# Output weights loaded piece by piece into the places of a finished activation, in a one-core AdaLN transformer block

## The chip, the cores and the metric

The kernel runs on one core of one Trainium2 chip. A core has TensorE (PE), which multiplies matrices, VectorE (DVE), ScalarE (ACT), GpSimd (POOL), and SyncE (SP), which here only issues DMA transfers. Each engine works through its own instructions in order, and they meet through semaphores. The metric is the device time of one execution in microseconds, lower being better.

## The reference

One adaptive-layernorm block over 2048 tokens of width 512, in fp32. A conditioning row `c` gives six rows of 512 numbers through `wmod`: `sa, ca, ga, sb, cb, gb`. Then

```python
h = layernorm(x) * (1 + ca) + sa
x = x + ga * attention(h)      # 16 heads of 128, causal; sum over heads of attn @ O_w, + O_b
h = layernorm(x) * (1 + cb) + sb
x = x + gb * experts(h)        # 64 experts, 4 per token, and two shared ones
```

`ga` and `gb` are first pushed away from zero (their magnitude is made at least 0.25). Only the attention half and the seam between the halves bear on this change.

## The kernel before

The normalised activation `hT` (512 x 2048, turned so that the width lies on partitions) is one tile of 4 MB. Attention runs over `steps` (L341): 16 heads of five steps each, written here as (head, step). A step s works on the query blocks `BATCHES[s]` (L339): 7; 6; 5 and 0; 4 and 1; 3 and 2, each of 256 queries. The order is written out by hand (`manual_schedule`): `merge` (L83) interleaves up to three streams of work by the columns of matmul that each holds, so that all come to their end together, and calls `marks` when a given share of the step has been issued. The streams of step n are

- the scores and softmax of step n+2 (`softmax_tile`, L368): matmuls of up to 1024 columns into `ps`, of which there are two buffers, the row maximum on DVE (L421), the exponential on ACT into `p` (L427), and later a normalisation on DVE (L397);
- the weighted values of step n (`weighted_values`, L463): matmuls of `v` with the turned probabilities `pt` into `po`, then a copy by ACT and a store by POOL's queue into the DRAM array `atd` (L489);
- fillers: the projections of the next head's k and q (`JOBS`, L343, 2048 columns each), the values of the next pair of heads (1024 each), and what a step adds.

At the end of a step `swap` (L595) issues 16 transfers on SP that exchange 32 x 32 block columns from `p` into `pt` (L451) for step n+2; at marks 0.55 and 0.8 of the next step DVE transposes the two halves of `pt` in place (L461). So a probability tile passes DVE, SP's queue, the DMA engines and DVE again before PE needs it.

Around the last two heads the kernel also prepares the second half of the block. The late rows `ga, sb, cb, gb` are made by `late_mod` (L525), four matmuls of 512 columns each from a 1 MB block of `wmod` that `load_mod` (L509) fetches: row 2 in step (14,4), rows 3 and 4 in (15,0), row 5 in (15,1). `gate` (L103) applies the magnitude rule, six DVE operations. The output weights `O_w` (4 MB) go to the place of `hT` once its last reader, `make_q` in (14,4), is done: in (15,0) POOL issues the loads of row 4's block, of `O_w` in four pieces (L631) and of row 5's block, and then multiplies the 16 heads' weights by `ga` (L636). `load_ab` (L539) fetches the stored attention of 15 heads for one block of 256 queries, and `begin_output(t)` (L555) sums 15 heads of output tile t (15 matmuls of 512 columns) into `parts[t]`; tiles 0 to 3 are made in steps (15,1) to (15,4). After the last step the head still missing is added for these four tiles (L896), and the other twelve tiles follow (L917).

Of the kernel before, what the change touches and what calls it, by code (L numbers as in the profile page):

```python
# [18 lines left out]
P = 128  # L19
# [4 lines left out]
def adaln_block_kernel(  # L24
# [99 lines left out]
    with ExitStack() as att:  # L124
# [1 line left out]
        acst = enter(tc.tile_pool(name="acst", bufs=1))  # L126
        psA = enter(tc.tile_pool(name="psA", bufs=2, space=PSUM))

        hT = hTp.tile([P, DC, N], F32, name="hT")
        causal = acst.tile([P, P], F32)  # L130
        make_causal_mask(nc, causal, mask_val=-1e30)
        qkb = acst.tile([P, 2, H], F32)
# [31 lines left out]
        def project(b, j, hd, pool, name):  # L164

            w = heads[hd][b]
            ps = psA.tile([P, 512], F32, name="pqk", tag="mm")
            for k in range(DC):
                nc.tensor.matmul(  # L169
                    out=ps,  # L170
                    lhsT=w[:, k, :],
                    rhs=hT[:, k, j * 512 : (j + 1) * 512],
                    start=(k == 0),
                    stop=(k == DC - 1),
                )
# [12 lines left out]
        with tc.tile_pool(name="pre", bufs=1) as pre, tc.manual_schedule():  # L188
# [92 lines left out]
            def place_x(b, half):  # L281
                tp = turns.pop((b, half))
                for j in range(2):
                    k = 2 * half + j
                    nc.scalar.activation(
                        hT[:, k, b * 512 : (b + 1) * 512], tp[:, j, :], AF.Identity,
                        scale=mod[1][:, k : k + 1], bias=mod[0][:, k : k + 1],
                    )

# [32 lines left out]
        def make_v(g, t):  # L322

            if t == 0:
                vts[g] = vp.tile([P, NT, HG * DH], F32, name="v")
            wv, vb = groups[g]
            ps = psA.tile([P, HG * DH], F32, name="pv", tag="mm")
            for k in range(DC):
                nc.tensor.matmul(  # L329
                    out=ps,  # L330
                    lhsT=hT[:, k, t * P : (t + 1) * P],
                    rhs=wv[:, k].rearrange("p i d -> p (i d)"),
                    start=(k == 0),
                    stop=(k == DC - 1),
                )
            nc.vector.tensor_add(vts[g][:, t, :], ps, vb)
# [9 lines left out]
            (("q", 3), ("v", 2), ("v", 3), ("v", 4)),  # L346
            (("q", 2), ("q", 0), ("v", 5)),
            (("q", 1), ("v", 6), ("v", 7)),
        )

        def blocks_of(s):
# [143 lines left out]
        def fillers(hd, s):  # L495
            out = []
            g = hd // HG
            for what, j in JOBS[s]:
                if what == "v":
                    if g + 1 < NG:  # L500
                        out.append((1024, lambda j=j: make_v(g + 1, (hd % HG) * NP + j)))
                elif hd + 1 < H:
                    f = make_k if what == "k" else make_q
                    out.append((2048, lambda j=j, f=f: f(hd + 1, j)))
            return out

        mods = {}

        def load_mod(i, queue):  # L509

            if i == 3:
                mods[i] = [ktp.tile([P, 512], F32, name="kt") for _ in range(DC)]
            elif i in (2, 4):
                both = [vow.tile([P, DC, HG, DH], F32, name="wv") for _ in range(2)]
                both = [w.rearrange("p k i d -> p (k i d)") for w in both]
                mods[i] = [both[k // 2][:, (k % 2) * D : (k % 2 + 1) * D] for k in range(DC)]
            else:
                four = [qkw.tile([P, DC, DH], F32, name=("wq", "wk")[k % 2]) for k in range(DC)]
                mods[i] = [w.rearrange("p k d -> p (k d)") for w in four]
            for k in range(DC):  # L520
                queue.dma_start(
                    out=mods[i][k], in_=wmod[k * P : (k + 1) * P, i * D : (i + 1) * D]
                )

        def late_mod(i, dst):  # L525

            pm = psA.tile([P, D], F32, name="pm", tag="mm")
            for k in range(DC):
                nc.tensor.matmul(
                    out=pm, lhsT=silc[:, k, :], rhs=mods[i][k], start=(k == 0), stop=(k == DC - 1)  # L530
                )
            if i == 4:
                nc.vector.tensor_scalar_add(dst, pm, 1.0)
            else:
                nc.vector.tensor_copy(dst, pm)

        abs_ = {}

# [16 lines left out]
        def begin_output(t):  # L555
# [4 lines left out]
            def one(hd):  # L560
                if hd == 0:
                    box.append(psA.tile([P, D], F32, name="psb", tag="mm"))
                nc.tensor.matmul(
                    out=box[0],
                    lhsT=abs_[t // 2][:, hd, (t % 2) * P : (t % 2 + 1) * P],
                    rhs=wo[:, hd, :],
                    start=(hd == 0),
                    stop=(hd == H - 2),
                )
# [32 lines left out]
        with tc.manual_schedule():  # L602
# [9 lines left out]
            for n, (hd, s) in enumerate(steps):  # L612
# [3 lines left out]
                    if hd % HG == 1 and hd // HG + 2 < NG:  # L616
                        groups[hd // HG + 2] = load_group(hd // HG + 2)
                fill = fillers(hd, s)
                if hd == H - 2 and s == 3:
                    load_mod(2, nc.sync)  # L620
                    load_mod(3, nc.sync)
                if hd == H - 2 and s == 4:
                    load_ab(0)
                    fill.append((2048, lambda: late_mod(2, ga)))
                if hd == H - 1 and s == 0:
                    mag = qkw.tile([P, DC, DH], F32, name="wq")
                    gate(mag.rearrange("p k d -> p (k d)"), ga)
                    load_mod(4, nc.gpsimd)
                    wo = hTp.tile([P, H, D], F32, name="hT")
                    for i in range(0, H, 4):  # L630
                        nc.gpsimd.dma_start(  # L631
                            out=wo[:, i : i + 4, :], in_=O_w[i : i + 4].rearrange("h p d -> p h d")
                        )
                    load_mod(5, nc.gpsimd)
                    for i in range(H):
                        nc.gpsimd.tensor_mul(wo[:, i, :], wo[:, i, :], ga)  # L636
                    fill += [
                        (2048, lambda i=i, dst=dst: late_mod(i, dst))
                        for i, dst in ((3, sb), (4, cb))
                    ]  # L640
                if hd == H - 1 and s == 1:
                    rest = [vow.tile([P, DC, HG, DH], F32, name="wv") for _ in range(2)]
                    rest = [w.rearrange("p (j k) i d -> p j (k i d)", j=2) for w in rest]
                    nc.sync.dma_start(out=rest[0][:, 0], in_=O_b.partition_broadcast(P))
                    for t in range(NE):
                        load_x_tile(t)
                    fill.append((2048, lambda: late_mod(5, gb)))
                if hd == H - 1 and s == 2:
                    gate(rest[1][:, 0], gb)
                if hd == H - 1 and s >= 1:  # L650
                    if s == 2:
                        place = pp.tile([P, PW], F32, name="p")[:, : (H - 1) * 2 * P]
                        load_ab(1, place.rearrange("p (h t) -> p h t", t=2 * P))
                    if s == 3:
                        load_ab(2)
                    if s == 4:
                        nc.vector.tensor_copy(ga, rest[0][:, 1])
                        nc.sync.dma_start(out=last3, in_=atd[H - 1, :, : (NE - 1) * P])
                        nc.sync.dma_start(out=ones, in_=atd[H - 1, :, (NE - 1) * P : NE * P])
# [227 lines left out]
    with tc.manual_schedule():  # L887
# [6 lines left out]
        for t in range(NE):  # L894
# [1 line left out]
            nc.tensor.matmul(  # L896
                out=ps,
                lhsT=last3[:, t * P : (t + 1) * P] if t < NE - 1 else ones,
                rhs=wo[:, H - 1, :],
                start=True,  # L900
                stop=True,
            )
# [3 lines left out]
        for t in range(NE, NT):  # L906
# [9 lines left out]
            for hd in range(H):  # L916
                nc.tensor.matmul(  # L917
                    out=ps,
                    lhsT=abs_[pr][:, hd, i * P : (i + 1) * P],
                    rhs=wo[:, hd, :],  # L920
                    start=(hd == 0),
                    stop=(hd == H - 1),
                )
# [423 lines left out]
```

## Time and profile before

| What | Value |
|---|---|
| Device time, median of 3 runs | 2510.37 us (2509.43 to 2513.41) |
| Profiled execution, device time | 2493.62 us |
| Profiled execution, span on the core | 2491.8 us |
| Mean granted TensorE clock there | 0.994 |
| PE, DVE, ACT, POOL busy | 2419.3, 1514.8, 656.0, 249.2 us |
| DMA volume, mean rate | 326.25 MB, 131 GB/s |
| L896 begins (end of attention) | 1772.2 us after the span's start |

All views are of the one profiled execution; its time is set beside its span, and the runs without the profiler are the ones that are compared between kernels. An engine's busy share is a mean over stages, so the page's 40 slices and shorter windows are read before the totals. In a timeline, the brackets after a line give the idle time of the engine just ahead of it and the event that ended it.

### The profile page before, as it was taken

Reading aid. Unit: us, or ns where it says so; the run is one execution under the profiler, and the core shown is the slowest. Engines: PE = TensorE matmul, PEld = TensorE weight load, DVE = VectorE, ACT = ScalarE, POOL = GpSimd, SP = SyncE. Lnnn points to the kernel's source line nnn. Section 1 sums busy time; section 2 is a strip of 40 time slices with the busy share of each in tenths; the row PEclk is TensorE's granted clock in tenths of the full one; section 3 lists DMA queues with packets and bytes.
Section 4 is the critical chain, followed back from the end, with each engine's and each line's share of the span. In section 5 each row is a group of like instructions: output and inputs, shape, how many; then the busy total and the mean of one; then the engine's idle time right before and its main releaser. Section 6 shows DMA issues by size and latency. Waiting matters only on the chain.

```text
span 2491.8 us, 26256 instructions
## 1 busy us (share of the span) xinstructions
PE 2419.3 (97%) x8525; PEld 1526.6 (61%) x8525; DVE 1514.8 (61%) x2966; ACT 656.0 (26%) x1476; POOL 249.2 (10%) x314
## 2 busy tenths in 40 slices
PE   7999999999999999999999999979999999999999
PEld 4666666666666666666666666545554476876844
DVE  4566666666666666666666666565465572553664
ACT  3233233332333323333233333221111221222200
POOL 0000000000000000000000000041000021111164
PEclk9999999999999999999999999989999999999999
DMA  4234434444344443444444444475524266878665
GB/s 140 62 91 107 116 95 110 107 103 109 90 121 102 97 120 94 112 111 103 109 97 121 104 101 108 109 227 135 164 81 152 89 180 209 250 213 251 198 191 161
DMA packets 224399, 326.25 MB, mean 131 GB/s; under 512 B 32100, under 2 KB 140680, under 8 KB 224264
## 3 DMA queue, kind: packets, MB, share of 16 engines
q1 hardware_dynamic: 195656, 246.96, 38.4%
q0 software_dynamic: 19392, 60.84, 8.1%
q10 hardware_dynamic: 9216, 16.78, 1.8%
q8 instruction: 69, 1.13, 0.2%
q14 instruction: 66, 0.54, 0.1%
HBM read 139.91 MB, written 41.94 MB: 73 GB/s over the span
## 4 chain that ended last, share of the span: by engine, by line
PE 67%; DVE 17%; SPq 6%; DMA 4%; issue 4%; ACT 1%; DVEq 0%; POOL 0%; ACTq 0%; POOLq 0%
PE pqk L169 12%; PE ps L408 12%; PE po L479 9%; DVE pt L461 7%; PE pso L917 6%; SPq L451 6%; PE pv L329 5%; PE pst L1064 5%; PE pse L1209 4%; PE psd L1126 4%; DVE nm L421 4%; DMA pt<-p 3%; PE psg L980 3%; DVE p L397 3%; PE psy L1230 2%
## 5 line engine op out<-in xcount | busy, mean ns | idle before, releaser
L427 ACT ACTIVATE p<-ps,nm 128x1024 f32<-128x1024 f32 (+7 forms) x384 | 331.9, 864 | 1040.5 <-DVE nm L425 368.4
L408 PE MATMUL ps<-kt,qt 128*128 128x512 f32 (+3 forms) x1280 | 535.2, 535 | 43.0 <-ACT p L427 42.1
L479 PE MATMUL po<-pt,v 128*128 128x256 f32 (+1 forms) x2304 | 567.5, 369 | 7.0 <-DVE pt L461 3.6
L479 PEld LDWEIGHTS po<-pt,v 128*128 128x128 f32 x2304 | 426.4, 191 | 220.3 <-issue 155.8
L421 DVE TENSOR_REDUCE nm<-ps 128x1 f32<-128x1024 f32 (+7 forms) x384 | 349.6, 910 | 91.1 <-PE ps L408 82.4
L461 DVE STREAM_TRANSPOSE pt<-pt 128x1664 f32<-128x1664 f32 (+2 forms) x160 | 318.0, 1988 | 64.2 <-DMA pt<-p 59.9
L408 PEld LDWEIGHTS ps<-kt,qt 128*128 128x128 f32 x1280 | 235.5, 191 | 193.3 <-issue 126.9
L420 DVE TENSOR_TENSOR ps<-ps,causal 128x128 f32<-128x128 f32 x256 | 74.4, 291 | 349.9 <-PE ps L408 349.9
L489 POOL DMA_DIRECT2D atd<-at x128 | 78.2, 612 | 1650.0 <-ACT at L488 1625.4
L329 PE MATMUL pv<-wv,hT 128*128 128x256 f32 x1024 | 240.4, 379 | 0.0
L169 PE MATMUL pqk<-hT,wk 128*128 128x512 f32 x512 | 232.7, 598 | 0.0
L169 PE MATMUL pqk<-hT,wq 128*128 128x512 f32 x512 | 231.4, 596 | 0.0
L397 DVE TENSOR_SCALAR p<-p,rs 128x1024 f32<-128x1024 f32 (+7 forms) x384 | 221.7, 606 | 9.3 <-DMA p<-atd 0.2
L329 PEld LDWEIGHTS pv<-wv,hT 128*128 128x128 f32 x1024 | 195.0, 190 | 31.0 <-issue 1.9
L917 PE MATMUL pso<-hT,v 128*128 128x512 f32 x384 | 173.7, 598 | 0.0
L169 PEld LDWEIGHTS pqk<-hT,wk 128*128 128x128 f32 x512 | 98.3, 193 | 102.9 <-issue 100.5
L169 PEld LDWEIGHTS pqk<-hT,wq 128*128 128x128 f32 x512 | 98.1, 192 | 97.1 <-issue 93.9
L1209 PE MATMUL pse<-wgu,xbT 128*128 128x256 f32 x512 | 121.1, 380 | 0.0
L917 PEld LDWEIGHTS pso<-hT,v 128*128 128x128 f32 x384 | 69.7, 191 | 71.4 <-issue 70.4
L1126 PE MATMUL psd<-wsd,hs 128*128 128x512 f32 x256 | 111.5, 593 | 0.0
L1209 PEld LDWEIGHTS pse<-wgu,xbT 128*128 128x128 f32 x512 | 93.9, 191 | 11.6 <-issue 1.0
L1192 POOL DMA_INDIRECT xb<-h2d,tok x64 | 64.8, 1012 | 300.8 <-PE tpx L1202 269.8
(264 smaller groups left out, 1943.3 us busy)
## 6 DMA issues: line engine op xcount, KB each, us to landing
pt<-p SPq DMA_DIRECT2D x768, 104.0 KB, 2.2
pt<-p SPq DMA_DIRECT2D x256, 124.0 KB, 2.3
pt<-p SPq DMA_DIRECT2D x256, 108.0 KB, 2.2
atd<-at POOLq DMA_DIRECT2D x128, 128.0 KB, 2.3
wgu<-in_L_ffn_Wg_dram SPq DMA_DIRECT2D x64, 256.0 KB, 4.3
wgu<-in_L_ffn_Wu_dram SPq DMA_DIRECT2D x64, 256.0 KB, 4.7
wd<-in_L_ffn_Wd_dram SPq DMA_DIRECT2D x64, 256.0 KB, 3.9
ybd<-y ACTq DMA_DIRECT2D x64, 256.0 KB, 3.7
```

Of the source, the lines that this page charges most:

```text
L169: nc.tensor.matmul(out=ps, lhsT=w[:, k, :], rhs=hT[:, k, j * 512 : (j + 1) * 512], start=(k == 0), stop=(k == DC - 1),)
L329: nc.tensor.matmul(out=ps, lhsT=hT[:, k, t * P : (t + 1) * P], rhs=wv[:, k].rearrange("p i d -> p (i d)"), start=(k == 0), stop=(k == DC - 1),
L397: nc.vector.tensor_scalar(cols[:, :, a:b], cols[:, :, a:b], rs[:, n : n + 1], None, ALU.mult)
L408: nc.tensor.matmul(out=ps[:, o : o + wo], lhsT=q, rhs=kts[hd, (c0 + o) // 512][:, :wo], start=True, stop=True,)
L421: nc.vector.tensor_reduce(nm[:, n : n + 1], ps[:, :w], AX.X, ALU.max, negate=True)
L427: nc.scalar.activation(rows[:, r0 + c0 // P : r0 + (c0 + w) // P], ps[:, :w].rearrange("q (r b k) -> q r b k", b=4, k=32), AF.Exp, bias=nm ...
L451: nc.sync.dma_start(out=pt[32 * b : 32 * (b + 1), a * w : (a + 1) * w], in_=pb[32 * a : 32 * (a + 1), b * w : (b + 1) * w],)
L461: nc.vector.transpose(part, part)
L479: nc.tensor.matmul(out=po if wide else po[:, P:], lhsT=vts[g][:, kt, hh * DH : (hh + 1) * DH], rhs=rows[:, r : r + last + 1 : last] if wid ...
L917: nc.tensor.matmul(out=ps, lhsT=abs_[pr][:, hd, i * P : (i + 1) * P], rhs=wo[:, hd, :], start=(hd == 0), stop=(hd == H - 1),)
L1126: nc.tensor.matmul(out=ps, lhsT=hsh[b, f][:, i * P : (i + 1) * P], rhs=wsd[:, f, :], start=(f == 0), stop=(f == NHC - 1),)
L1209: nc.tensor.matmul(out=ps, lhsT=xts[e][:, k, :], rhs=weights[e][:, k].rearrange("p i h -> p (i h)"), start=(k == 0), stop=(k == DC - 1),)
```

## The change: four tiles for hT, earlier rows, earlier output tiles

`hT` becomes four tiles, one for each 512 tokens. In head 14, which has no values to make for a next pair, the projections are listed apart (`JOBS14`): all three remaining q jobs stand in step 3. As soon as the last reader of one of the four tiles has been issued, a 1 MB piece of `O_w` is loaded into its place on SP: three pieces within (14,3), the fourth in (14,4). The multiplication by `ga` moves from POOL to DVE, two heads at a time, at marks of (14,3), (14,4) and (15,0).

For this, `ga` has to exist earlier: rows 2 and 3 are made in heads 3 and 5, their blocks of `wmod` loaded into the places of `parts[1]` to `parts[3]` and `gb`, with the gate of `ga` in (4,1). Row 4's block is loaded in (13,1) and row 5's in (14,1); both rows are made in (14,4). All these loads are on SP. The stored attention of block 0 is loaded in (14,0), (14,1) and (14,4), that of block 1 in (15,1) into a `pt` buffer instead of a `p` buffer, that of block 2 in (15,2). Output tiles 0 to 3 are begun in (15,0) to (15,3), so that (15,4) is left with the weighted values alone. Instructions of other stages keep their order.

```diff
-        hT = hTp.tile([P, DC, N], F32, name="hT")
+        hTs = [hTp.tile([P, DC, 512], F32, name=f"hT{j}") for j in range(NB)]
...
+        JOBS14 = (
+            (("k", 0), ("k", 1)), (("k", 2), ("k", 3)), (("q", 3),),
+            (("q", 2), ("q", 0), ("q", 1)), (),
+        )
...
-            for what, j in JOBS[s]:
+            for what, j in JOBS[s] if hd < H - 2 else JOBS14[s]:
...
+        spare = parts[1:] + [gb]
         mods = {}
-        def load_mod(i, queue):
-            if i == 3:
-                mods[i] = [ktp.tile([P, 512], F32, name="kt") for _ in range(DC)]
-            elif i in (2, 4):
+        def load_mod(i):
+            if i == 5:
                 both = [vow.tile([P, DC, HG, DH], F32, name="wv") for _ in range(2)]
...
             else:
-                four = [qkw.tile([P, DC, DH], F32, name=("wq", "wk")[k % 2]) for k in range(DC)]
-                mods[i] = [w.rearrange("p k d -> p (k d)") for w in four]
+                mods[i] = spare
...
+        MOD_LOADS = {(3, 1): 2, (5, 1): 3, (13, 1): 4, (14, 1): 5}
+        MOD_ROWS = {(3, 3): ((2, ga),), (5, 3): ((3, sb),), (14, 4): ((4, cb), (5, gb))}
+        PLACES = (3, 2, 0, 1)
+        WO_LOADS = {(14, 3): (0, 1, 2), (14, 4): (3,)}
+        WO_SCALES = {
+            (14, 3): [(0.75, 0)],
+            (14, 4): [(0.1, 2), (0.3, 4), (0.45, 6), (0.65, 8)],
+            (15, 0): [(0.1, 10), (0.3, 12), (0.45, 14)],
+        }
+        wos = {}
+        def load_wo(i):
+            wos[i] = hTp.tile([P, 4, D], F32, name=f"hT{PLACES[i]}")
+            nc.sync.dma_start(
+                out=wos[i], in_=O_w[4 * i : 4 * i + 4].rearrange("h p d -> p h d")
+            )
+        def scale_wo(i):
+            for j in (i, i + 1):
+                w = wos[j // 4][:, j % 4, :]
+                nc.vector.tensor_mul(w, w, ga)
...
-                if hd == H - 2 and s == 3:
-                    load_mod(2, nc.sync)
-                    load_mod(3, nc.sync)
-                if hd == H - 2 and s == 4:
-                    load_ab(0)
-                    fill.append((2048, lambda: late_mod(2, ga)))
+                if (hd, s) in MOD_LOADS:
+                    load_mod(MOD_LOADS[hd, s])
+                if (hd, s) in MOD_ROWS:
+                    fill += [(2048, lambda m=m: late_mod(*m)) for m in MOD_ROWS[hd, s]]
+                if (hd, s) == (4, 1):
+                    gate(parts[1], ga)
+                if (hd, s) in ((14, 0), (14, 1)):
+                    load_ab(0, heads=((0, 4), (4, 8)) if s == 0 else ((8, 12), (12, 14)))
+                if (hd, s) == (14, 4):
+                    load_ab(0, heads=((14, 15),))
+                    for t in range(NE):
+                        load_x_tile(t)
                 if hd == H - 1 and s == 0:
-                    mag = qkw.tile([P, DC, DH], F32, name="wq")
-                    gate(mag.rearrange("p k d -> p (k d)"), ga)
-                    load_mod(4, nc.gpsimd)
-                    wo = hTp.tile([P, H, D], F32, name="hT")
-                    for i in range(0, H, 4):
-                        nc.gpsimd.dma_start(
-                            out=wo[:, i : i + 4, :], in_=O_w[i : i + 4].rearrange("h p d -> p h d")
-                        )
-                    load_mod(5, nc.gpsimd)
-                    for i in range(H):
-                        nc.gpsimd.tensor_mul(wo[:, i, :], wo[:, i, :], ga)
-                    fill += [
-                        (2048, lambda i=i, dst=dst: late_mod(i, dst))
-                        for i, dst in ((3, sb), (4, cb))
-                    ]
-                if hd == H - 1 and s == 1:
                     rest = [vow.tile([P, DC, HG, DH], F32, name="wv") for _ in range(2)]
...
-                    for t in range(NE):
-                        load_x_tile(t)
-                    fill.append((2048, lambda: late_mod(5, gb)))
-                if hd == H - 1 and s == 2:
+                if hd == H - 1 and s == 1:
                     gate(rest[1][:, 0], gb)
-                if hd == H - 1 and s >= 1:
-                    if s == 2:
-                        place = pp.tile([P, PW], F32, name="p")[:, : (H - 1) * 2 * P]
-                        load_ab(1, place.rearrange("p (h t) -> p h t", t=2 * P))
-                    if s == 3:
-                        load_ab(2)
+                    place = ptp.tile([P, PW], F32, name="pt")[:, : (H - 1) * 2 * P]
+                    load_ab(1, place.rearrange("p (h t) -> p h t", t=2 * P))
+                if hd == H - 1 and s == 2:
+                    load_ab(2)
...
-                    fill += begin_output(s - 1)
+                if hd == H - 1 and s < NE:
+                    fill += begin_output(s)
                 streams = [weighted_values(hd, s, turned.pop(n)), fill]
+                if (hd, s) == (14, 3):
+                    fill[:] = [fill[0], (0, lambda: load_wo(0)), (0, lambda: load_wo(1)),
+                               fill[1], (0, lambda: load_wo(2)), fill[2]]
+                if (hd, s) == (14, 4):
+                    load_wo(3)
...
-                marks = []
+                marks = [(f, lambda i=i: scale_wo(i)) for f, i in WO_SCALES.get((hd, s), ())]
```

Everywhere else `hT[:, k, ...]` becomes the matching slice of one of the four tiles, and `wo[:, hd, :]` becomes `wos[hd // 4][:, hd % 4, :]`.

More of the change, by code (lines that the diff above doesn't have):

```diff
@@ L171, in project @@
                     lhsT=w[:, k, :],
-                    rhs=hT[:, k, j * 512 : (j + 1) * 512],
+                    rhs=hTs[j][:, k, :],
                     start=(k == 0),
@@ L285, in place_x @@
                     nc.scalar.activation(
-                        hT[:, k, b * 512 : (b + 1) * 512], tp[:, j, :], AF.Identity,
+                        hTs[b][:, k, :], tp[:, j, :], AF.Identity,
                         scale=mod[1][:, k : k + 1], bias=mod[0][:, k : k + 1],
@@ L330, in make_v @@
                     out=ps,
-                    lhsT=hT[:, k, t * P : (t + 1) * P],
+                    lhsT=hTs[t // 4][:, k, (t % 4) * P : (t % 4 + 1) * P],
                     rhs=wv[:, k].rearrange("p i d -> p (i d)"),
@@ L517, in load_mod @@
             else:
-                four = [qkw.tile([P, DC, DH], F32, name=("wq", "wk")[k % 2]) for k in range(DC)]
-                mods[i] = [w.rearrange("p k d -> p (k d)") for w in four]
+                mods[i] = spare
             for k in range(DC):
-                queue.dma_start(
+                nc.sync.dma_start(
                     out=mods[i][k], in_=wmod[k * P : (k + 1) * P, i * D : (i + 1) * D]
@@ L535, in late_mod @@
                 nc.vector.tensor_copy(dst, pm)
+        MOD_LOADS = {(3, 1): 2, (5, 1): 3, (13, 1): 4, (14, 1): 5}
[10 more added lines that the diff above has]
+            wos[i] = hTp.tile([P, 4, D], F32, name=f"hT{PLACES[i]}")
+            nc.sync.dma_start(
+                out=wos[i], in_=O_w[4 * i : 4 * i + 4].rearrange("h p d -> p h d")
[4 more added lines that the diff above has]
+                nc.vector.tensor_mul(w, w, ga)
         abs_ = {}
@@ L565, in one @@
                     lhsT=abs_[t // 2][:, hd, (t % 2) * P : (t % 2 + 1) * P],
-                    rhs=wo[:, hd, :],
+                    rhs=wos[hd // 4][:, hd % 4, :],
                     start=(hd == 0),
@@ L644, in adaln_block_kernel @@
                     nc.sync.dma_start(out=rest[0][:, 0], in_=O_b.partition_broadcast(P))
-                    for t in range(NE):
-                        load_x_tile(t)
-                    fill.append((2048, lambda: late_mod(5, gb)))
+                if hd == H - 1 and s == 1:
+                    gate(rest[1][:, 0], gb)
+                    place = ptp.tile([P, PW], F32, name="pt")[:, : (H - 1) * 2 * P]
+                    load_ab(1, place.rearrange("p (h t) -> p h t", t=2 * P))
                 if hd == H - 1 and s == 2:
-                    gate(rest[1][:, 0], gb)
-                if hd == H - 1 and s >= 1:
-                    if s == 2:
-                        place = pp.tile([P, PW], F32, name="p")[:, : (H - 1) * 2 * P]
-                        load_ab(1, place.rearrange("p (h t) -> p h t", t=2 * P))
-                    if s == 3:
-                        load_ab(2)
[L656 to L659, printed above, removed]
-                    fill += begin_output(s - 1)
-                streams = [weighted_values(hd, s, turned.pop(n)), fill]
+                    load_ab(2)
+                if hd == H - 1 and s == 4:
+                    nc.vector.tensor_copy(ga, rest[0][:, 1])
+                    nc.sync.dma_start(out=last3, in_=atd[H - 1, :, : (NE - 1) * P])
+                    nc.sync.dma_start(out=ones, in_=atd[H - 1, :, (NE - 1) * P : NE * P])
+                if hd == H - 1 and s < NE:
+                    fill += begin_output(s)
+                streams = [weighted_values(hd, s, turned.pop(n)), fill]
+                if (hd, s) == (14, 3):
[3 more added lines that the diff above has]
+                    load_wo(3)
                 if n + 2 < len(steps):
                     streams.insert(0, softmax_work(n + 2))
-                marks = []
+                marks = [(f, lambda i=i: scale_wo(i)) for f, i in WO_SCALES.get((hd, s), ())]
                 if n + 1 < len(steps):
@@ L898, in adaln_block_kernel @@
                 lhsT=last3[:, t * P : (t + 1) * P] if t < NE - 1 else ones,
-                rhs=wo[:, H - 1, :],
+                rhs=wos[(H - 1) // 4][:, (H - 1) % 4, :],
                 start=True,
@@ L919, in adaln_block_kernel @@
                     lhsT=abs_[pr][:, hd, i * P : (i + 1) * P],
-                    rhs=wo[:, hd, :],
+                    rhs=wos[hd // 4][:, hd % 4, :],
                     start=(hd == 0),
```

## The prediction

> **What bounds the kernel now.** I read four views in this order. First the page: TensorE (PE) is busy 97% of the span, so any gain must come from the few slices where it isn't.
>
> ```profile
> span 2491.8 us, 26256 instructions
> ...
> PE   7999999999999999999999999979999999999999
> ...
> POOL 0000000000000000000000000041000021111164
> PEclk9999999999999999999999999989999999999999
> DMA  4234434444344443444444444475524266878665
> ```
>
> A slice is 62.3 us. Apart from the first, the one weak PE slice is number 27 (1620 to 1682 us): there PE shows 7 and its clock 8, POOL wakes up, DMA reaches 7. Next, busy times in windows of 20 us (PE, PEld, DVE, ACT, POOL, granted clock, DMA share, GB/s):
>
> ```profile
> 1640.00:1660.00 20.00, 16.59 (x53) 9.71 (x53) 17.41 (x34) 5.52 (x14) 8.80 (x14) 0.93 0.88 250
> 1660.00:1680.00 20.00, 10.50 (x32) 6.05 (x31) 10.21 (x16) 2.67 (x8) 13.62 (x12) 0.76 1.00 297
> ```
>
> PE loses half of the second window while DMA is full. Third, the PE timeline, which names the stalls (idle time before, and releaser, in brackets):
>
> ```profile
> 1605.86 1.06 PE L479 MATMUL po<-pt,v 128*128 128x256 f32 x2 [2.10 <-ACT at L488]
> 1606.72 4.97 PE L169 MATMUL pqk<-hT,wq 128*128 128x512 f32 x8
> ...
> 1646.67 0.67 PE L479 MATMUL po<-pt,v 128*128 128x256 f32 x2 [1.25 <-issue]
> ...
> 1656.81 0.82 PE L408 MATMUL ps<-kt,qt 128*128 128x256 f32 x2 [2.16 <-ACT p L427]
> 1657.42 5.22 PE L529 MATMUL pm<-wv,silc 128*128 128x512 f32 x8
> ...
> 1678.24 3.42 PE L408 MATMUL ps<-kt,qt 128*128 128x512 f32 x4 [7.38 <-ACT p L427]
> ...
> 1723.69 1.77 PE L408 MATMUL ps<-kt,qt 128*128 128x512 f32 x4 [2.27 <-ACT p L427]
> ```
>
> ACT is only the messenger. Fourth, the timelines of DVE and POOL and of the SP queue, and the DMA issues, say why:
>
> ```profile
> 1665.76 1.98 DVE L461 STREAM_TRANSPOSE pt<-pt 128x1728 f32<-128x1728 f32 x1 [2.40 <-DMA pt<-p]
> ...
> 1674.37 1.98 DVE L461 STREAM_TRANSPOSE pt<-pt 128x1728 f32<-128x1728 f32 x1 [4.23 <-DMA pt<-p]
> ```
>
> ```profile
> 1671.31 15.28 POOL L636 TENSOR_TENSOR hT<-hT,ga 128x512 f32<-128x512 f32 x12 [1.33 <-DMA hT<-in_L_attn_O_w_dram]
> ```
>
> ```profile
> 1616.48 2.04 SPq L521 DMA_DIRECT2D wv<-in_L_wmod_dram  x4
> 1618.56 1.85 SPq L521 DMA_DIRECT2D kt<-in_L_wmod_dram  x4
> ```
>
> ```profile
> hT<-in_L_attn_O_w_dram POOLq DMA_DIRECT2D x4, 1024.0 KB, 19.4
> ```
>
> In step (15,0) (head 15, step 0) some 8 MB are wanted at once: O_w 4 MB and two late weight blocks 2 MB from POOL, two heads' worth of stored attention 2 MB from SP. The swap transfers pt<-p, normally 2.2 us, take 10.03 and 8.58 us in the chain of waits; DVE's in-order transposes wait for them, so the next score maxima, exponentials and score matmuls do too.
>
> **What the Trainium skill says.** (1) "DMA: Bandwidth & Descriptors", section "Issuing engines are not separate DMA queues": transfers from any engine share the same 16 engines. The trace agrees: POOL's loads slow SP's swaps from 2.2 to 10 us. (2) "SBUF — State Buffer", "Who interferes with whom": a GpSimd operation that reads SBUF contends with DVE operations of two SBUF inputs or in a two-port mode. The trace agrees: while POOL multiplies, a normalise pair takes DVE 3.06 us (1679.96) against 1.08 (1565.62). (3) "VectorE: DVE Perf Modes", the errata section, gives (N+151)/0.96 ns for an fp32 tensor_tensor, 691 ns at 512; the trace has 0.69 us (L572). POOL takes 1298 ns for the same shape. (4) "TensorE: Matmul & The Clock Gate", "What's actually happening": an idle window of about 3.4 us halves PE's clock. The trace shows the loss even after 2.1 us: eight records in 4.97 us against 3.60.
>
> **The change, part by part.** Unit: 2048 columns of matmul take 3.43 us (chain of waits, L169 x8), so 1.677 us per 1000. A step's columns are the scores of the step two ahead (3968, 3456, 3328, 3328, 3328 for s = 0 to 4), the weighted values (the same numbers), and fillers. I take the stretch from the first matmul of (14,3) at 1601.78 to the first output matmul L896 at 1772.23: 170.45 us.
>
> Before, in columns: 11392, 10880, 11392, 16512, 14336, 11008, 11008, or 19.1 + 18.2 + 19.1 + 27.7 + 24.0 + 18.5 + 18.5 = 145.1 us. The excess is 25.4. By step starts (1625.09, 1643.43, 1678.24, 1707.50, 1734.7, 1753.23): 4.2 in (14,3), 0.1 in (14,4), 15.7 in (15,0), 1.6 in (15,1), 3.2 in (15,2), -0.3 after that, 0.8 at L896.
>
> After: one q job goes from (14,4) to (14,3); two late rows leave the stretch for heads 3 and 5; the output tiles move one step earlier. Columns 13440, 10880, 14976, 14464, 14336, 11008, 3328: 22.5 + 18.2 + 25.1 + 24.3 + 24.0 + 18.5 + 5.6 = 138.2. Now the excess of each step:
>
> - (14,3): 4.2 as before. Its stall at 1605.86 comes from the unchanged short step (14,2). The first three O_w pieces (3 MB) follow the swap on SP, near 1616.5. The two late blocks at that place landed by 1623.6: 2 MB in 7.1 us. So about 3.6 us per piece, the first in by 1622. DVE reaches its multiply (mark 0.75) near 1624.5: no wait, with 2 us to spare. The last piece lands near 1628, before the swap of (15,0) at about 1633.
> - (14,4): 0.3. Eight multiplies come in, 8 x 0.69 = 5.5 us, and one more row copy (0.7). DVE was busy 12.6 of the 20 us from 1620. Score matmuls have two buffers, so a late maximum isn't felt at once. x tiles, the fourth piece and one head's attention (2.1 MB) follow the swap on SP and land before the next swap.
> - (15,0): 3.3. Between the end of the second late row and the second transpose of (15,0) DVE had copy, transpose, maximum, normalise, transpose: 8.5 us (1637.98 to 1646.49) against 7.4 us of PE work, hence the 1.25. Now a multiply pair (1.3) stands in between: 2.5 us. Clock loss after it between 0 (as at 1723.69) and 1.6 (as at 1657.42); I take 0.8. The bulk loads, POOL's 20 us of multiplies, the gate of ga (3.5 us of DVE) and the 14 us that they cost are gone. The other three multiply pairs (4.1 us) fit into 25 us of PE work.
> - (15,1): 0.5, with the gate of gb (3.1 us) now here; DVE is through it by about 7 us, the third score chunk comes at 9.
> - (15,2): 0.9. The 2.27 goes: the exponential waited for a p buffer whose turn the attention load had taken, behind a swap; the load now sits in a pt buffer.
> - L896: 0.8 as now. (15,4) has only 5.6 us left to hide the store and reload of the last head's blocks: in the trace the PE end of (15,3) is 1753.0, the reload is issued at 1756.08 and lands 2.8 later, 5.9 us in all. The cover is just enough.
>
> Sum 10.0. Stretch 148.2, so -22.3; the two late rows cost 2 x 3.43 = +6.9 in heads 3 and 5, which are PE-bound. Their 1 MB loads fall between swaps, where SP idles some 7 us of each step (a swap is issued in 10 of 17 to 18 us). The gate in (4,1) (3.5 us) falls where DVE now idles 4.63 us before 550.65: nothing. It would cost up to 3 us if that gap were used. Total -15.4: span 2491.8 to 2476.4, profiled execution 2493.6 to 2478.2. The median of the runs is 2510.37, 16.7 above the profiled one; I carry the difference over unchanged: **2495 us**. Splitting hT costs nothing: the same bytes in the same places, the same matmuls.
>
> Both ends of what the trace doesn't show. O_w multiply pairs on DVE: 0 on the path to all 14 that lie in (14,4) and (15,0), 9.6 us. First piece late: 0 to 10 us (landing in 19.4 us as the POOL loads did, less 2 us of slack). L896: 0 to 2 us. Moved rows: -1 to +3, since they may also fill existing gaps.
>
> **The rivals.**
> - DVE becomes the bound in (14,4) and (15,0): the 14 multiplies all show (9.6 us instead of 1.3). For: 12.6 + 5.5 + 0.7 = 18.8 us of DVE work in a step of 18.2. Against: (15,0) has 25 us. -15.4 + 8.3 = -7: 2503.
> - More goes than I count: the stall at (14,3) and that at (15,0) both vanish. 4.2 + 3.3 more: 2487.5. Against: (14,2) isn't touched.
> - Slower: O_w pieces land late and DVE, in order, waits at the multiply ahead of transposes and maxima. If each piece took 19.4 us one after the other, the third would land at 1675 where DVE wants it at 1645.5 with 2 us of slack: 27.7 lost, 15.4 won, 2523. It decides from 15 us per piece on. Against: 3.6 us per MB at the same place of the same queue.
> - The change doesn't do what it says: the timed runs hold 16.7 us that the profile doesn't show; if those absorb what idle time gives back, 2509.
>
> **How the numbers follow.** Forecast 0.68 (own spread 2490 to 2501), DVE bound 0.14, more 0.08, slower 0.06, nothing 0.04. Range 2487 to 2504: it takes in the case of more and the middle of the DVE case; late pieces, nothing and the tails stay out, about 0.2. A measurement tells some 0.2% (5 us) from no change. Faster: 0.68 + 0.10 + 0.08 = 0.86; same 0.04 + 0.04 = 0.08; slower 0.06.
>
> **What would show it.** Right: windows at 1640 to 1700 with PE full, POOL without TENSOR_TENSOR, pt<-p back at 2.2 us, the DVE line of the O_w multiply without a DMA wait, a PE stall of 2 to 3 us at the start of (15,0), (15,4) only 5.6 us long. Wrong: DVE waiting for an O_w transfer, PE waiting at L896 over 2 us, new stalls in heads 3 to 5, or a span above 2487.

## The result, and the profile after

| | median, us | runs | lowest to highest |
|---|---|---|---|
| before | 2511.89 | 4 | 2509.43 to 2513.75 |
| after | 2493.09 | 4 | 2491.56 to 2494.97 |

The ratio is 0.9929 with a 95% interval of 0.9917 to 0.9942: by the medians 18.8 us faster, by the interval (times 2511.89) between 14.6 and 20.8. The forecast was 2495.

The page of the changed kernel, its slices of 62.3 us:

```profile
span 2493.2 us, 26246 instructions
...
PE   7999999999999999999999999899999999999989
...
POOL 0000000000000000000000000000100011111163
PEclk9999999999999999999999999999999999999999
DMA  4234444444443443444434444565423267778564
```

The hole in slice 27 is gone from PE and from its clock, and GpSimd no longer works there. Two slices now show an 8: number 26, with (14,3), and number 39, close to the end, of which more below. The windows around (15,0) (PE, PEld, DVE, ACT, POOL, clock, DMA share, GB/s):

```profile
1640.00:1660.00 20.00, 18.92 (x62) 11.00 (x60) 16.64 (x27) 5.01 (x12) 1.54 (x2) 1.00 0.68 175
1660.00:1680.00 20.00, 19.19 (x59) 11.02 (x59) 17.41 (x31) 5.27 (x13) 1.00 (x1) 1.00 0.60 161
```

PE was busy 10.50 us of the second window at a clock of 0.76; it is now busy 19.19 at full clock, and DMA, which was full, is at 0.60. The PE timeline of the changed kernel has all the stalls over 0.6 us that are left from (14,3) to the seam (the first output matmul of the last head's blocks, L915, formerly L896):

```profile
1616.14 0.79 PE L484 MATMUL po<-pt,v 128*128 128x256 f32 x2 [2.90 <-ACT at L493]
1616.72 5.24 PE L169 MATMUL pqk<-hT,wq 128*128 128x512 f32 x8
...
1658.34 1.98 PE L413 MATMUL ps<-kt,qt 128*128 128x512 f32 x4 [1.08 <-ACT p L432]
...
1661.13 0.67 PE L484 MATMUL po<-pt,v 128*128 128x256 f32 x2 [0.81 <-issue]
...
1758.18 3.00 PE L915 MATMUL pso<-hT,last 128*128 128x512 f32 x6 [0.68 <-DMA last<-atd]
```

The first pair is the stall of (14,3) and the clock lost after it (eight records in 5.24 us instead of 3.60). Then 1.9 us at the entry of (15,0), and 0.68 at the seam, where PE waits for the reload of the last head's blocks.

The length from the first matmul of (14,3) to the seam is 1758.18 - 1611.25 = 146.9 us; it was 170.45. The seam comes 14.05 us earlier. But the span is 1.4 us longer than the span of before, 2493.2 against 2491.8. What follows the seam took 735.0 us instead of 719.6, and the PE and DVE timelines near the end show where:

```profile
2415.13 0.69 DVE L1152 TENSOR_TENSOR acc<-acc,psd 128x512 f32<-128x512 f32 x1 [14.59 <-remote]
```

```profile
2422.52 5.20 PE L999 MATMUL psg<-h2T,wsu 128*128 128x512 f32 x8 [12.05 <-DVE sig L988]
```

DVE waits 14.59 us for something that the trace doesn't name, and PE 12.05 us for DVE. The change touches nothing there. This was the first question for the experiments: between these two profiles that wait hides the whole gain.

### The profile page after: what moved, and what is told of

Read it like the earlier page. It is cut to its first block, busy times and chain, and to the rows that moved or that the text cites. A ratio compares the mean times of both kernels' runs of the same rounds, so it can differ in the third digit from the quotient of the medians.

```text
span 2493.2 us, 26246 instructions
## 1 busy us (share of the span) xinstructions
PE 2420.1 (97%) x8525; PEld 1524.6 (61%) x8525; DVE 1518.9 (61%) x2982; ACT 656.7 (26%) x1476; POOL 223.5 (9%) x286
## 4 chain that ended last, share of the span: by engine, by line
PE 58%; issue 18%; DVE 13%; SPq 5%; DMA 2%; ACT 1%; POOL 1%; another core or an unknown queue 1%; DVEq 0%; ACTq 0%; POOLq 0%
PE pqk L169 9%; PE ps L413 9%; PE po L484 7%; PE pso L936 6%; DVE pt L466 5%; PE pv L329 5%; PE pst L1083 5%; PE pse L1228 4%; SPq L456 4%; PE psd L1145 4%; PE psg L999 3%; DVE nm L426 3%; PE psy L1249 2%; DVE p L402 2%; DMA pt<-p 1%
```

## The experiments

The runs were made in three sessions of four kernels, e1 to e4, e5 to e8 and e9 to e12, the first and the third on one chip, the second on another; within a session they share the runs of the kernel before (2511.01, 2510.74 and 2496.62 us, medians of 47, 43 and 24). To compare stretches between profiles I measure from a score record in head 14 that all kernels have at full clock (128x384, 1584.43 in before, 1593.87 in after) to the seam. I call this the late stretch: 187.80 us before, 164.31 after. "Rest" is what follows the seam. The "hole" is the stretch of (15,0) in which PE of the kernel before stands still.

| run | ratio to before | interval | late stretch | rest |
|---|---|---|---|---|
| e1 before again | 1.0004 | 0.9995-1.0013 | 188.07 | 736.2 |
| e2 multiplies on GpSimd | 0.9965 | 0.9954-0.9975 | 170.44 | 731.2 |
| e3 pieces late | 1.0018 | 1.0010-1.0025 | 183.97 | 734.8 |
| e4 q job moved | 0.9918 | 0.9899-0.9938 | 159.70 | 731.2 |
| e5 pt buffer | 0.9986 | 0.9977-0.9996 | 187.64 | 734.3 |
| e6 attention early | 1.0003 | 0.9990-1.0015 | 192.06 | 736.9 |
| e7 no multiplies | 0.9997 | 0.9988-1.0006 | 188.23 | 733.5 |
| e8 outputs late | 1.0004 | 0.9996-1.0013 | 179.65 | 735.4 |
| e9 rows alone | 1.0036 | 1.0024-1.0047 | 188.48 | 720.2 |
| e10 quarter of O_w | 1.0003 | 0.9993-1.0013 | 187.21 | 725.8 |
| e11 q job moved, again | 0.9930 | 0.9912-0.9948 | 159.66 | 721.6 |
| e12 after again | 0.9934 | 0.9917-0.9951 | 163.97 | 720.2 |

**e1: the kernel before, unchanged.**

> The kernel before, unchanged, profiled once more. In the two profiles at hand the seam (first matmul of L896, in the changed kernel L915) is at 1772.2 and 1758.2 us, 14.1 apart, but the rest of the span is 719.6 us before and 735.0 after, because PE is idle for 12.05 us in the last 100 us of the changed kernel while DVE and ACT wait for something the profile doesn't name. Theory A, the idle time near the end comes and goes from one execution to the next, whatever the change: a second profile of the kernel before can have a rest of about 735, and a time near 2510. Theory B, it belongs to the changed program alone: rest 719.6 +- 1 again and a time near 2494. Both: seam at 1772 +- 1.5, ratio of times 1.000 +- 0.001.

In its PE timeline, at the place where after waits:

```profile
2438.18 5.89 PE L980 MATMUL psg<-h2T,wsu 128*128 128x512 f32 x8 [10.65 <-issue]
```

So the wait is in the kernel before too, and it is the first profile of before that lacked it: 736.2 - 719.6 = 16.6 us longer is what follows the seam, against 16.7 between that profile and its timed runs. The wait and the clock lost after it (5.89 us instead of 3.70) make up 12.8 of them, and 3.0 more are clock lost near 1980 us, after a stall of 2.98 us that both profiles have. Theory A of the expectation holds. The seam is at 1775.25, beyond the 1772 +- 1.5 expected, because the part ahead of head 14 ran longer; the late stretch is the same. All eight profiles of the first two sessions have the wait (5.6 to 15.9 us of idle PE at this place). In the third session it is at most 1.83, against the 10 us expected for e12, the changed kernel again:

```profile
2447.78 3.70 PE L999 MATMUL psg<-h2T,wsu 128*128 128x512 f32 x8 [1.68 <-DVE sig L988]
```

In that session before runs at 2496.62 and after at 2481.43. The wait comes and goes with the session, for both kernels, and the first and the third session were on the same chip. Its cause isn't settled; no run was made for it.

**e2: the multiplies of the O_w pieces on GpSimd.**

```diff
-                nc.vector.tensor_mul(w, w, ga)
+                nc.gpsimd.tensor_mul(w, w, ga)
```

> The changed kernel with the O_w multiplies back on POOL, at the same marks. Theory (prediction): a multiply pair between DVE's two transposes of (15,0) costs PE about 1.3 us there, and without it the stall at the first weighted values of (15,0) is 0 to 0.3 us instead of 0.81 and that at the score matmul before it 0 instead of 1.08: 1 to 2 us faster than the changed kernel. Rival: POOL's multiplies (1.3 us each) hold DVE's normalise and the stores of at behind them, so stalls of 1 to 4 us appear in (14,3) to (15,0): slower than the changed kernel by 2 to 5 us. Seam against the changed kernel's 1758.2: theory 1756 to 1757.5, rival 1760 to 1763.

The theory failed and the rival was right in kind: the late stretch is 6.1 us longer than in after, where 2 to 5 were expected. The timelines of GpSimd and VectorE in e2:

```profile
1643.38 9.81 POOL L563 TENSOR_TENSOR hT<-hT,ga 128x512 f32<-128x512 f32 x8
```

```profile
1642.94 11.40 DVE L402 TENSOR_SCALAR p<-p,rs 128x1024 f32<-128x1024 f32 x2
```

A pair of normalisations that takes 1.35 us takes 11.40, as long as GpSimd's eight multiplies run. The Trainium skill ("SBUF — State Buffer", "Who interferes with whom") says that a VectorE instruction in a two-port mode and one of GpSimd block each other, the one issued second until the other is through. The trace agrees that it can be a full stop, and a longer one: the first of the two normalisations, begun 0.44 us ahead of GpSimd's multiplies, took 10.80 us and outlasted all eight of them. It isn't always so: in before a pair took 3.06 us while GpSimd ran twelve multiplies in a row. What makes the difference isn't shown. In e2 the swap behind the pair is then late, and PE stalls 3.94 us at 1656.77 and loses clock. Putting the multiplies on DVE is therefore a part of the gain, not a cost that has to be hidden.

**e3: all four O_w pieces at the start of (14,4).**

```diff
-            (14, 3): [(0.75, 0)],
-            (14, 4): [(0.1, 2), (0.3, 4), (0.45, 6), (0.65, 8)],
+            (14, 4): [(0.1, 0), (0.1, 2), (0.3, 4), (0.45, 6), (0.65, 8)],
...
-                    load_wo(3)
+                    for i in range(4):
+                        load_wo(i)
```

> The changed kernel with all four O_w pieces loaded at the start of (14,4), as one tile would have forced, and multiplied from mark 0.1 of (14,4) on. Theory (timing of the O_w transfers decides): the multiplies of heads 0 to 3 wait on DVE for a transfer that is queued behind the swap of (15,0), 10 us or more, and DVE holds transposes and maxima behind it: PE idles 8 to 15 us in (14,4) and (15,0), seam at 1766 to 1773, most of the gain gone. Rival (the gain came from POOL no longer multiplying and from the rows made in heads 3 and 5, not from when O_w comes): seam within 3 us of 1758.2.

DVE and PE in e3:

```profile
1664.11 2.50 DVE L562 TENSOR_TENSOR hT<-hT,ga 128x512 f32<-128x512 f32 x4 [19.98 <-DMA hT<-in_L_attn_O_w_dram]
```

```profile
1671.02 2.50 PE L413 MATMUL ps<-kt,qt 128*128 128x512 f32 x4 [15.44 <-ACT p L432]
```

This is the case of the prediction's slower rival: one in-order wait of DVE for a weight piece holds all that is queued behind it. The late stretch is 19.7 us longer than in after; the theory was right in kind and expected less, 8 to 15 us of idle PE, where 15.44 and 2.64 were measured.

**e4 and e11: one q job of (14,3) in (14,2).** In after the largest stall left is at the entry of (14,3), behind the short step (14,2).

```diff
-            (("k", 0), ("k", 1)), (("k", 2), ("k", 3)), (("q", 3),),
-            (("q", 2), ("q", 0), ("q", 1)), (),
+            (("k", 0), ("k", 1)), (("k", 2), ("k", 3)), (("q", 3), ("q", 2)),
+            (("q", 0), ("q", 1)), (),
...
-                    fill[:] = [fill[0], (0, lambda: load_wo(0)), (0, lambda: load_wo(1)),
-                               fill[1], (0, lambda: load_wo(2)), fill[2]]
+                    fill[:] = [(0, lambda: load_wo(0)), (0, lambda: load_wo(1)), fill[0],
+                               (0, lambda: load_wo(2)), fill[1]]
```

and the mark of the fifth multiply pair from 0.65 to 0.85.

> The changed kernel with q job 2 moved from (14,3) to the short step (14,2), the first two pieces loaded at the start of (14,3), and the multiply pair at mark 0.65 of (14,4) moved to 0.85, behind the second transpose. Theory: the stall of 2.90 us at the first weighted values of (14,3), and 1.6 us of lost clock after it, come from (14,2) having only 14.6 us of matmuls, too few to cover its swap and transposes; with 18.0 us both go, and the stalls of 1.08 and 0.81 at (15,0) shrink to under 0.5 in all: seam 5 to 6 us earlier, 1752 to 1753.5, time ratio to before about 0.990. Rival: the stall follows the swap of (14,3), which depends on when DVE finishes, and comes back at another step: seam within 2 us of 1758.2.

> The changed kernel with one q job of (14,3) in (14,2) and the first two O_w pieces at the start of (14,3), again, beside the changed kernel on the same chip. If its advantage is the stall at the entry of (14,3) and the clock lost after it, the first matmul of L915 is again 4 to 5 us earlier from the start of head 14 than in the changed kernel, and the median 2 to 5 us lower; if it was a matter of the run, the two are the same.

> The changed kernel as it is, beside the run with the moved q job: 0.9925 to 0.993 of before, with PE idle for some 10 us ahead of L999 as in its first profile.

PE in e4:

```profile
1620.44 0.70 PE L484 MATMUL po<-pt,v 128*128 128x256 f32 x2 [0.95 <-ACT at L493]
...
1659.89 0.67 PE L484 MATMUL po<-pt,v 128*128 128x256 f32 x2 [0.81 <-issue]
```

The stall of 2.90 is 0.95, without loss of clock. At (15,0) the stall of 1.08 is gone with the multiply pair that stood ahead of the second transpose, and 0.81 stays, where under 0.5 was expected. The late stretch is 4.6 us shorter than in after in e4 (5 to 6 expected) and 4.3 in e11 against e12 (4 to 5 expected). The ratio of e12, 0.9934, is near the 0.9925 to 0.993 expected. The medians are 2489.97 against 2493.09, and, within one session, 2478.33 against 2481.43, each 3.1 lower. The intervals of the ratios overlap, so the traces carry this, not the times. It is the best version found.

**e5: the kernel before with the attention load in a pt buffer.**

```diff
-                        place = pp.tile([P, PW], F32, name="p")[:, : (H - 1) * 2 * P]
+                        place = ptp.tile([P, PW], F32, name="pt")[:, : (H - 1) * 2 * P]
```

> The kernel before with one edit: the stored attention of the second pair of tiles goes into a pt buffer instead of a p buffer, as in the changed kernel. Theory (the prediction's step on (15,2)): the stall of 2.27 us ahead of the score matmul at 1723.69 exists because an exponential waits for the p buffer whose turn the load has taken. It should go, nothing else change: the first matmul of L896 about 2.3 us earlier counted from the start of head 14, the run at 0.999 of before. Rival: the step is behind by its DVE work, so the stall moves to the next score matmul or stays, and L896 moves by less than 0.7 us.

The stall of 2.27 us in (15,2) is gone, with nothing over 0.6 us in its place. From the matmul that ends the hole of (15,0) to the seam e5 needs 1777.44 - 1684.48 = 92.96 us, e1 94.63: 1.7 gained of 2.3. The whole late stretch is only 0.4 shorter, as the way to the end of the hole came out 1.2 longer in this profile. By the whole stretch the rival's mark (under 0.7) is met; the trace, where the stall is gone and none has come in its place, speaks for the theory.

**e6: the kernel before with the attention of heads 0 to 13 loaded in (14,0) and (14,1).**

```diff
+                if (hd, s) in ((14, 0), (14, 1)):
+                    load_ab(0, heads=((0, 4), (4, 8)) if s == 0 else ((8, 12), (12, 14)))
...
-                    load_ab(0)
+                    load_ab(0, heads=((14, 15),))
```

> The kernel before with one edit: the first pair of tiles' stored attention of heads 0 to 13 (1.75 MB) is loaded in (14,0) and (14,1), as in the changed kernel, instead of ahead of (15,0). Some 6 MB are then wanted in (15,0) instead of 8. Theory (the flood of transfers slows the swaps): the swaps of 10.03 and 8.58 us get shorter in proportion, to some 7, and the 15.7 us that (15,0) loses become 9 to 12; L896 comes 4 to 7 us earlier from the start of head 14; ratio 0.9975 to 0.9985. Rival (GpSimd's multiplies hold VectorE back, the transfers are secondary): less than 1.5 us. Rival 2 (only this load matters, since it stands on SP's own queue ahead of the swaps, while GpSimd's loads do not delay them): 12 us or more.

None of the three expectations foresaw this: the late stretch is 4 us longer. Of that, 1.3 are there before the hole, 0.4 come in the hole and 1.5 are clock lost after the stall of (15,2). Windows of e1 and of e6:

```profile
1640.00:1660.00 20.00, 16.85 (x57) 9.96 (x56) 17.00 (x28) 4.00 (x9) 7.74 (x12) 1.00 0.84 238
1660.00:1680.00 20.00, 11.53 (x34) 6.36 (x32) 10.29 (x18) 2.83 (x8) 12.41 (x12) 0.78 1.03 293
```

```profile
1640.00:1660.00 20.00, 16.45 (x55) 9.59 (x53) 16.34 (x27) 3.76 (x8) 7.54 (x12) 1.00 0.53 133
1660.00:1680.00 20.00, 10.43 (x34) 6.24 (x34) 9.57 (x17) 2.97 (x9) 11.52 (x12) 0.84 1.03 283
```

The 2 MB are missing from the first window (133 GB/s for 238); in the second, where PE stands, DMA is as full as before. In the kernel before they had been through ahead of the hole, so they don't cause it.

**e7: the kernel before without GpSimd's multiplies.**

```diff
-                    for i in range(H):
-                        nc.gpsimd.tensor_mul(wo[:, i, :], wo[:, i, :], ga)
```

> The kernel before without the sixteen GpSimd multiplies of the output weights by ga: that part of the computation is left out, all loads stay. Theory (the flood): (15,0) still loses 12 to 15 of its 15.7 us, since the transfers are the same; L896 1 to 4 us earlier from the start of head 14; ratio 0.9985 to 0.9995. Rival (the multiplies hold VectorE at the shared SBUF access): the normalise pair is back at 1.1 us, (15,0) loses 5 us or less; L896 10 us earlier; ratio 0.996.

The kernel leaves out the multiplication by `ga`. The normalise pair takes 1.08 us instead of 3.06, but PE still stalls 7.20 us (7.28 in e1), and nothing is gained: the rival (10 us) is refuted, and the 1 to 4 us of the theory don't come either. In the kernel before these multiplies slowed an engine that was waiting for a swap anyway; in e2, where the swap is prompt, the same operation costs 6 us.

**e10: the kernel before with a quarter of O_w.**

```diff
-                    for i in range(0, H, 4):
+                    for i in range(0, 4, 4):
```

and `i % 4`, `hd % 4` where the pieces are used; the weights of twelve heads are left out.

> The kernel before with only the first of the four O_w transfers: 1 MB instead of 4, and the weights of heads 0 to 3 are used for all heads (the other twelve heads' output weights are left out); sixteen multiplies and all matmuls stay. Theory (the bytes on the 16 DMA engines delay the swaps): 3 MB of 6 stay in (15,0), the swaps end within 5 us, (15,0) loses 5 us or less of its 15.7; L896 10 to 13 us earlier from the start of head 14, ratio 0.995 to 0.996. Rival (the order of the queues or GpSimd's multiplies hold the step, not the bytes): L896 within 3 us, ratio 0.999 or more.

The expectation failed: the late stretch is 0.9 shorter than in e1, not 10 to 13. DMA issues of e10 (KB each, median us to landing, from 1650 to 1680):

```profile
pt<-p SPq DMA_DIRECT2D x16, 108.0 KB, 8.4
...
hT<-in_L_attn_O_w_dram POOLq DMA_DIRECT2D x1, 1024.0 KB, 12.3
wq<-in_L_wmod_dram POOLq DMA_DIRECT2D x2, 256.0 KB, 14.3
```

In before the swap took 8.9 in the same window. The delay isn't in proportion to the bytes: 3 MB of bulk loads beside the swap make it as late, nearly, as 6 MB. The busy share of the DMA engines in before and in e10, from 1650 to 1680 in slices of 0.75 us, suggests why:

```profile
DMA  3539899999999999999999999999999999999992
```

```profile
DMA  9983566999999999999999999999983000000000
```

The swap's last transfer lands at 1673.97 in before and at 1673.98 in e10. In e10 the DMA engines fall idle just then, so 3 MB are enough to go beside the swap to its end; in before they stay busy for 5 us more, so a part of the 6 MB only comes after the swap. That less than 3 MB would let it land earlier is not shown. With none beside it the same swap lands in 2.2 us in e12.

**e9: the kernel before with the late rows alone moved**, loads, rows and the gate of ga as in the change; O_w stays in one load on GpSimd's queue.

> The kernel before with the late rows alone moved as in the changed kernel (rows 2 and 3 and the gate of ga in heads 3 to 5, rows 4 and 5 in (14,4)); O_w stays one load and sixteen multiplies on GpSimd at (15,0). The load there falls from 6 MB to 4, and its matmul work from 11392 to 7296 columns (12.2 us). Theory (the time of the transfers, not the work of the engines, sets the length of (15,0)): its 34.8 us shrink with the bytes, to some 27; the first matmul of L896 about 8 us earlier from the start of head 14, of which 6.9 is handed to heads 3 and 5: ratio 0.999 to 1.0015. Rival (the moved rows bring the main part of the gain): L896 14 us or more earlier, ratio 0.996 or less.

The theory failed (8 us earlier were expected), and so did the rival. The kernel is slower than before by 0.24 to 0.47%. PE in e9:

```profile
1682.03 0.79 PE L408 MATMUL ps<-kt,qt 128*128 128x128 f32 x2 [11.51 <-ACT p L427]
1690.86 3.78 PE L408 MATMUL ps<-kt,qt 128*128 128x512 f32 x4 [7.61 <-ACT p L427]
```

The 6.9 us of rows leave the late stretch and its length doesn't change (188.48): PE has less to do and waits longer for the same swap, which takes 9.0 us beside the 4 MB of O_w. Heads 3 and 5 pay for the rows, and nothing comes back.

**e8: the changed kernel with the output tiles in steps 1 to 4 again.**

```diff
-                if hd == H - 1 and s < NE:
-                    fill += begin_output(s)
+                if hd == H - 1 and s > 0:
+                    fill += begin_output(s - 1)
```

> The changed kernel with the first output tiles back in steps 1 to 4 of the last head, so that (15,0) has 7296 columns (12.2 us of matmul) instead of 14976 (25.1). Theory (the extra PE work in (15,0) is what hides the six O_w multiplies on VectorE there): VectorE's work in (15,0), its usual 12 plus 4.1 of multiplies, no longer fits, (15,0) or (15,1) loses 3 to 4 us more; the wait of 0.68 at the seam goes as (15,4) is longer; the first matmul of L915 2.5 to 3.5 us later from the start of head 14; ratio 1.0010 to 1.0015 against the changed kernel. Rival (the multiplies are hidden by themselves, the step of the output tiles is of no account): within 0.7 us. Rival 2 (the longer last step helps): L915 0.7 us earlier.

The whole gain is gone: ratio to before 1.0004, the late stretch 15.3 us longer than in after; 2.5 to 3.5 were expected. PE, and the chain of waits in e8:

```profile
1669.06 0.72 PE L413 MATMUL ps<-kt,qt 128*128 128x256 f32 x2 [2.03 <-ACT p L432]
...
1672.16 3.78 PE L413 MATMUL ps<-kt,qt 128*128 128x512 f32 x4 [1.54 <-ACT p L432]
...
1682.41 2.98 PE L413 MATMUL ps<-kt,qt 128*128 128x512 f32 x4 [2.48 <-ACT p L432]
...
1754.21 0.67 PE L484 MATMUL po<-pt,v 128*128 128x256 f32 x2 [2.78 <-DVE pt L466]
```

```profile
1672.97 0.60 SPq L456
1674.25 0.60 SPq L456
1674.89 0.59 SPq L456
1676.16 2.22 DMA pt<-p
1678.70 1.98 DVE pt L466
...
1734.14 10.62 DMA v<-atd
1745.96 0.59 SPq L456
1746.60 0.60 SPq L456
1749.78 2.20 DMA pt<-p
1752.20 1.92 DVE pt L466
```

Transfers are prompt here (2.2 us), and yet (15,0) is too short. Its chain is the swap: sixteen issues on SP of 0.63 us each, one transfer, one transpose, then maximum and exponential. With 12.2 us of matmul beside it PE stalls 6.05 us and loses some 4 us of clock. That the chain from the start of the swap on holds SP's issues and no multiply corrects the theory I had put down: the last and largest stall, which ends at 1682.41, is not set by VectorE's multiplies. They have a part in the second stall (1.54), though: the score maximum for which it waits stands on DVE behind four multiplies.

```profile
1667.68 2.49 DVE L563 TENSOR_TENSOR hT<-hT,ga 128x512 f32<-128x512 f32 x4
```

No run separates the two. The last part, 2.78 us and another 1.5 of clock, is a second effect that I had not seen: the load of the last attention pair (`v<-atd`) waits until the first pair's output tiles are done, and on SP's queue it stands ahead of the swap of (15,4). With outputs a step later it holds that swap up. So some 4 of the 15.3 us are this order of the queue, and about 10 the missing cover in (15,0).

## Why the prediction came out right, point by point

- **The stretch.** 146.9 us against 148.2. The matmul work was 138.2 by the column count, so 8.7 are excess where 10.0 were forecast: (14,3) 2.90 + 1.64 + 0.2 = 4.7 (4.2); (15,0) 1.9 (3.3, with no loss of clock after it); (14,4), (15,1) and (15,2) nothing over 0.6 (0.3, 0.5 and 0.9); the seam 0.68 (0.8). The other 1.4 us lie in smaller gaps that I haven't placed.
- **The rows.** Forecast +6.9 in heads 3 and 5. From one profile of each the head 14 record moved by 9.4; the mean of the six profiles of kernels without the move is 1587.4, of the eight with it 1595.4: 8.1, where single profiles spread by 4 to 6 us, so 6.9 isn't excluded.
- **The sum.** -23.5 + 8.1 = -15.4, the forecast. Both terms are 1.2 us larger than forecast, and that they cancel is luck. The medians differ by 18.8 and, in the third session, by 15.2. The 3.4 us between -15.4 and -18.8 aren't placed; the rest after the seam alone varies from 731.2 to 736.9 over the profiles of the first two sessions.
- **The 16.7 us carried over.** Right, and the riskiest step, as no view of the prediction showed where they lay: e1 shows that they lie after the seam, 12.8 of them at a wait that the profile of before happened not to have. The mark "wrong if the span is above 2487" was badly set for this reason; it was passed with the forecast intact.
- **O_w in time.** The pieces were there when DVE came (its first multiply, at 1634.57, shows no wait). e3 shows the price of the other case: 19.7 us for one step's delay; the rival said 27.7 (27.2 by its own terms: three pieces of 19.4 us from 1616.5 on, against 1645.5 and 2 us of slack).
- **DVE as the bound.** No: of the seven pairs in (14,4) and (15,0) one shows, as forecast, the one between DVE's two transposes (1.08 us, which goes in e4 where the pair stands behind them). With all the multiplies on GpSimd the late stretch is 6.1 us longer.
- **The p buffer.** e5 confirms that stall's cause; it gives 1.7 of 2.3.
- **What the working misjudged.** It explained the hole of (15,0) by "some 8 MB" wanted at once. Of these the 2 MB of attention were harmless (e6), GpSimd's multiplies too (e7), and taking half of the other 6 MB away brought 0.9 us (e10). And it gave the output tiles no value of their own: they appear as columns that move from one step to another, at no cost and no gain, and are used only to say that (15,0) has 25 us. In e8 the loads are out of (15,0) and the swaps are prompt, and PE still stalls there: that the 14 us go with the loads alone, as the prediction had it, is not so. Without the output tiles in (15,0) no gain in time is left. The forecast came out right because the change brought in the tiles with the rest.

How the 23.5 us come about can be read from before to e9 to e8 to after. Rows alone: the late stretch +0.7. Then the loads out of (15,0), with all else that e8 has of the change (the pt buffer, DVE's multiplies, the earlier attention, the moved q jobs; e9 to e8): -8.8. Then the output tiles a step earlier (e8 to after): -15.3, of which some 4 are the order of SP's queue. The parts need each other: rows alone make the kernel slower, rows and loads come out even with before, and only all three gain.

## What to carry to other kernels

A step in a pipelined loop has a latency chain (here sixteen issues, a transfer, a transpose, a maximum, an exponential) and an amount of matmul work; in the steps measured here the longer of the two set the length. Taking work out of a step whose chain is longer gained nothing in e9; shorten the chain and bring work in from later steps, in the same edit. And before one profile is compared with another, repeat the kernel before: a wait that comes and goes (up to 15.9 us here) can be as large as the change.

## What the hardware showed that was not expected

- VectorE's normalise pair took 11.40 us, instead of 1.35, while GpSimd ran eight multiplies of 128x512 (e2); beside twelve of them in before another pair took 3.06.
- Stalls of PE at the entry of (14,3) cost clock: after 2.24 us in e9, 2.41 in e1 and 2.90 in after the next eight records took 5.24 to 5.29 us instead of 3.60, after 0.95 in e4 just 3.60. So there a stall that shrinks from 2.90 to 0.95 gives back nearly twice its difference. The length of the stall alone doesn't decide: in (15,2) 2.27 us in before and 3.06 in e9 cost nothing, and after 2.31 in e6 four records took 3.32 us instead of 1.77. And one stall of 2.98 us after the seam, which both have, cost nothing in before (at 1976.28) and 3.0 us in e1 (at 1979.29). What decides isn't shown.
- The wait near the end: 5.6 to 15.9 us in the first two sessions, under 2 in the third, for both kernels, and on one chip in the first and the third.
- Bulk loads of 3 MB beside a swap made its transfers land after 8.4 us, 6 MB after 8.9, none after 2.2 (e10, before, e12).
